# A graph network's adjacency built from subtiles of 5 nodes with one tile of 128 edges each, their rows gathered once a chunk from a table of overlapping rows

## The chip, the cores and the metric

The kernel runs on one NeuronCore of a Trainium2 chip. The metric is the device time of one execution in microseconds, as the median of 11 runs. The engines are called as the profile calls them: PE (TensorE; PEld is its weight load), DVE (VectorE), ACT (ScalarE), POOL (GpSimd) and SP (SyncE, which here only issues DMAs). Sixteen DMA engines move the data.

## The reference

Four graph layers run over the same graph, each with a residual and a layer norm. There are N = 6250 nodes with 128 features, and E = 100000 edges, whose list is sorted by destination.

```python
edge_index = jnp.stack([src, dst])
x = _layernorm(x + _L0_gnn_ref(x, edge_index, L0_gnn_W_l, L0_gnn_b_l, L0_gnn_W_r), axis=-1)
x = _layernorm(x + _L1_gnn_ref(x, edge_weight1, ..., src, dst, edge_type_8), axis=-1)
x = _layernorm(x + _L2_gnn_ref(x, edge_index, ...), axis=-1)
x = _layernorm(x + _L3_gnn_ref(x, edge_index, edge_attr_16, ...), axis=-1)
```

Layer 0, in whose stage the change lies, takes the mean of `x[src]` over the edges of each destination, multiplies it with `W_l`, adds a bias and `x @ W_r`, and normalizes the rows. Layer 1 sums messages by relation, layer 2 runs five gated steps, each with a sum over the same edges, and layer 3 is an edge network with a sum by source.

## The kernel before

The kernel has two routes. A preparation (`gnn_kernel`) looks at the edge list, works out tables, and sets a flag; a regular graph like this one then takes the route `even`, any other the route `general`.

**Dense and sparse nodes.** The 6250 nodes are 49 tiles of 128 (`NT`). They go in steps of 768 nodes: 4 tiles, called a chunk, are summed by a dense product, and 2 tiles by lists of edges. There are 8 dense chunks of 512 destinations (`DW`) and 17 listed tiles. The sum of a dense chunk is a product with its adjacency, a count matrix of 128 source rows by 49 source tiles by 512 destinations in bf16. Layer 0 builds these 8 matrices, uses each once (`dense0`), and stores it in DRAM (`stored`, `adj_d`) for layer 2's five steps.

**How an adjacency is built.** A chunk is cut into 43 subtiles of `U = 12` destination nodes. The edges into one subtile fit into `US = 256` places, that is two tiles of 128 edges. For each edge the preparation has written a record of two numbers into `rec_d`: a key of source tile and destination, and the source's place in its tile. `block_load` reads for a block of up to 11 subtiles (`SU`) the starts of the edges (`start_d`, a register load on SP) and then the 256 records of each subtile, one DMA each; all of this is on SP's queue. `block_keys` subtracts the subtile's offset (L931) and compares the places with 0 to 127 into one-hots `ohs` (L935), both on DVE. `hot_keys` makes for each edge tile a one-hot `ohk` over 600 columns (50 source tiles by 12 nodes, L943, DVE). `subtile` multiplies the two on PE (L958): two edge tiles by two halves of 300 columns make four matmuls, which add up in a PSUM tile of two banks, of which there are two. ACT copies the 600 columns into the chunk's `stage` (L960).

**What stands beside it.** For a listed tile, `fetch0` gathers 128 messages by an indirect DMA on POOL (L754, 10 buffers, 8 ahead), `hot0` makes a one-hot on DVE (L1002), and `sparse0` multiplies them (L1011). `dense0` multiplies three bf16 parts of x with the stage, 147 matmuls of 512 columns a chunk (L980). `post` does the rest of layer 0 for a chunk, and then layer 1's products `fhw` (L1095) with their stores. `counts` works out the edges per node.

**What sets the order.** Each engine works its queue in order. In layer 0 that order is written by hand: pieces of work get a place in a list (`events`), counted in chunks, and `play` issues them sorted by it. A chunk's adjacency is built in one such period, while `dense0` works on the chunk before, so there are nine periods: the first only builds, the last only uses. In the preparation the order comes from a scheduler when the kernel is built. It puts `rec_d<-rec` on SP's queue behind 11 of the 13 loads of x, whose parts are then made by ACT and POOL and written to `x_in`. The first instructions of `even` wait for the last of these writes.

Of the kernel before, what the change touches and what calls it, by code (L numbers as in the profile page):

```python
# [34 lines left out]
U = 12  # L35
US = 256
SU = 11
DW = 512
SLOTS = 18
NU = (N + U - 1) // U  # L40
RL = 200
RQ = EC // RL
QR = P - 1
NQ = 5 * QR
KH = (NT + 1) // 2
# [617 lines left out]
def even(ctx: ExitStack, tc: tile.TileContext, a, out, rec_d, start_d, list_d, x_in, ends):  # L663
# [115 lines left out]
    with tc.tile_pool(name="f0", bufs=1) as l0, \  # L779
# [5 lines left out]
        start = l0.tile([1, NQ + P], I32, name="start")  # L785
# [23 lines left out]
        def list_load(i):  # L809
            t, n = sparse[i][0], len(sparse[i])  # L810
            dst_ls[i] = dst_l = l0.tile([P, 2, SLOTS], I32, tag="dst_l", bufs=3, name=f"dst_l{i}")
            _, at = nc.values_load_multi_w_load_instructions(
                start[0:1, NQ + t:NQ + t + n], engines=[ET.SP], min_val=0, max_val=E,
                skip_runtime_bounds_check_because="counts of edges, none above their number")
            for j in range(n):
                for to, k in ((src_l[:, 2 * i + j, :], 0), (dst_l[:, j, :], 1)):
                    nc.sync.dma_start(to, list_d[k, bass.ds(at[j], SLOTS * P)].rearrange("(p s) -> p s", p=P))
# [82 lines left out]

        iota_k = l0.tile([P, KH * 2 * U], FP16, name="iota_k")
        nc.gpsimd.iota(iota_k, pattern=[[1, KH * 2 * U]], base=0, channel_multiplier=0,
                       allow_small_or_imprecise_dtypes=True)
        iota_u = l0.tile([P, SU], F32, name="iota_u")
        nc.gpsimd.iota(iota_u, pattern=[[1024, SU]], base=0, channel_multiplier=0,
                       allow_small_or_imprecise_dtypes=True)


        each = -(-DW // U)
        blocks = [(d, ts[0] * P // U + u, min(SU, each - u)) for d, ts in enumerate(dense) for u in range(0, each, SU)]  # L910
        recs, keys, ohss, stages, hot, msgs, sums, aggT, parts = ({} for _ in range(9))

        def block_load(i):
            if i >= len(blocks):
                return
            d, b, n = blocks[i]
            recs[b] = rec = l0.tile([P, SU, 2, 2], F32, tag="recs", bufs=4, name=f"recs{b}")
            _, at = nc.values_load_multi_w_load_instructions(
                start[0:1, b:b + n], engines=[ET.SP], min_val=0, max_val=E,
                skip_runtime_bounds_check_because="counts of edges, none above their number")  # L920
            for u in range(n):
                nc.sync.dma_start(rec[:, u, :, :].rearrange("p j r -> p (j r)"),
                                  rec_d[bass.ds(at[u], US), :].rearrange("(p j) r -> p (j r)", p=P))

        def block_keys(i):
            if i >= len(blocks):
                return
            d, b, n = blocks[i]
            rec = recs.pop(b)
            keys[b] = key = l0.tile([P, SU, 2], F32, tag="key", bufs=3, name=f"key{b}")  # L930
            nc.vector.scalar_tensor_tensor(key[:, :n, :], rec[:, :n, :, 0], float(-1024 * b),  # L931
                                           iota_u[:, :n].unsqueeze(2).to_broadcast([P, n, 2]),
                                           op0=ALU.add, op1=ALU.subtract)
            ohss[b] = ohs = l0.tile([P, 2 * SU, P], BF16, tag="ohs", bufs=2, name=f"ohs{b}")
            nc.vector.tensor_tensor(ohs[:, :2 * n, :], iota_h.unsqueeze(1).to_broadcast([P, 2 * n, P]),  # L935
                                    rec.rearrange("p u j r -> p (u j) r")[:, :2 * n, 1:2].to_broadcast([P, 2 * n, P]),
                                    op=ALU.is_equal)

        def hot_keys(b, u):
            ks = []  # L940
            for j in range(2):
                ohk = l0.tile([P, 2 * KH * U], BF16, tag="ohk", bufs=5, name=f"ohk{b}_{u}_{j}")
                nc.vector.tensor_scalar(ohk, iota_k, keys[b][:, u, j:j + 1], None, op0=ALU.is_equal)  # L943
                ks.append(ohk)
            hot[b, u] = ks

        def subtile(d, b, u, after):

            if after:
                hot_keys(*after)  # L950
            if d not in stages:
                stages[d] = l0.tile([P, 2 * KH, DW], BF16, tag="stage", bufs=2, name=f"stage{d}")
            c = (b + u) * U - dense[d][0] * P
            w = min(U, DW - c)
            p = ps(f"adj_p{b}_{u}", "adj", 2, 1024)
            for j, ohk in enumerate(hot.pop((b, u))):
                for q in range(2):
                    nc.tensor.matmul(p[:, q * 512:q * 512 + KH * U], ohss[b][:, 2 * u + j, :],  # L958
                                     ohk[:, q * KH * U:(q + 1) * KH * U], start=(j == 0), stop=(j == 1))
            nc.scalar.copy(stages[d][:, :, c:c + w].rearrange("p (q b) d -> p q b d", q=2),  # L960
                           p.rearrange("p (q n) -> p q n", q=2)[:, :, :KH * U]
                           .rearrange("p q (b d) -> p q b d", d=U)[:, :, :, :w])
# [27 lines left out]
        def fetch0(k):  # L990
            if k >= len(hots):
                return
            i, j = hots[k]
            msgs[k] = msg = l0.tile([P, 3 * D], BF16, tag="msg", bufs=10, name=f"m0_{k}")
            gather(msg, x_in, src_l[:, i, j:j + 1])
# [8 lines left out]
        def sparse0(k):  # L1004
            i, j = hots[k]
            fetch0(k + 8)
# [102 lines left out]
        with tc.manual_schedule(engines=FOUR):  # L1109
            list_load(0)  # L1110
            block_load(0)
            list_load(1)
            block_load(1)
            load_weights()
            list_locs(0)
            block_keys(0)
            for k in range(8):
                fetch0(k)
            for k in range(6):
                hot0(k)  # L1120
            order = [(d, b, u) for d, b, n in blocks for u in range(n)]
            hot_keys(*order[0][1:])
# [3 lines left out]
            for d in range(len(dense)):  # L1126
                mine = [o for o in order if o[0] == d]
                for k, (_, b, u) in enumerate(mine):
                    t = d + (k + 0.5) / len(mine)
                    g = order.index((d, b, u))  # L1130
                    nxt = order[g + 1][1:] if g + 1 < len(order) else None
                    i = [x[1] for x in blocks].index(b)
                    if u == 0 and i:
                        events.append((t - 1e-6, lambda i=i: block_load(i + 1)))
                    if u == 7:
                        events.append((t - 2e-6, lambda i=i: block_keys(i + 1)))
                    events.append((t, lambda d=d, b=b, u=u, nxt=nxt: subtile(d, b, u, nxt)))
# [945 lines left out]
def gnn_kernel(ctx: ExitStack, tc: tile.TileContext, a, out):  # L2083
# [4 lines left out]
    rec_d = dram.tile([E + US, 2], F32, name="rec_d")  # L2088
    start_d = dram.tile([NQ + P], I32, name="start_d")
# [7 lines left out]
    with tc.tile_pool(name="prep", bufs=1) as prep, \  # L2097
# [13 lines left out]
        for p0, p1 in ((0, 112), (112, EP)):  # L2111
# [9 lines left out]
        NR = NQ // QR + 1  # L2121
        node = prep.tile([P, NR * P], F32, name="node")
        nc.gpsimd.iota(node[:, :(NR - 1) * P], pattern=[[U * QR, NR - 1], [U, P]], base=0, channel_multiplier=0,
                       allow_small_or_imprecise_dtypes=True)
        nc.gpsimd.iota(node[:, (NR - 1) * P:], pattern=[[P, P]], base=0, channel_multiplier=0,
                       allow_small_or_imprecise_dtypes=True)
        own = prep.tile([P, NR], F32, name="own")
        nc.gpsimd.iota(own[:, :NR - 1], pattern=[[U * QR, NR - 1]], base=0, channel_multiplier=U,
                       allow_small_or_imprecise_dtypes=True)
        nc.gpsimd.iota(own[:, NR - 1:], pattern=[[0, 1]], base=0, channel_multiplier=P,  # L2130
                       allow_small_or_imprecise_dtypes=True)
# [29 lines left out]
        p_t = psum.tile([P, 512], F32, name="p_t")  # L2161
# [6 lines left out]
        nc.sync.dma_start(start_d[:NQ].rearrange("(r c) -> r c", c=QR), at_i[:NR - 1, :QR])  # L2168
        nc.sync.dma_start(start_d[NQ:].rearrange("(o n) -> o n", o=1), at_i[NR - 1:, :])

# [8 lines left out]
        nc.vector.tensor_scalar(miss, p_t[:NR, P:2 * P], float(E * U // N) / U, float(E), op0=ALU.mult, op1=ALU.min)  # L2179
# [7 lines left out]
        nc.vector.tensor_scalar(most, most, float(NR - 1), float(SLOTS * P - US), op0=ALU.is_equal, op1=ALU.mult)  # L2187
        nc.vector.tensor_scalar(most, most, float(US), None, op0=ALU.add)
        room = prep.tile([NR, QR], F32, name="room")
        nc.vector.tensor_sub(room, at[:, 1:], at[:, :QR])  # L2190
# [54 lines left out]
        q = pre("q")  # L2245
        nc.vector.tensor_scalar(q, d_f[:, :EC], 1.0 / U, -(U - 1) / (2.0 * U), op0=ALU.mult, op1=ALU.add)
        nc.vector.tensor_scalar(q, q, BIG, None, op0=ALU.add)
        nc.vector.tensor_scalar(q, q, -BIG, None, op0=ALU.add)
        v = pre("v")
# [81 lines left out]
```

## Time and profile before

| what | value |
| --- | --- |
| median of 11 runs | 7677.67 us (7668.8 to 7686.42) |
| profiled execution, its own time | 7692.67 us |
| span of its trace | 7690.9 us |
| mean granted TensorE clock | 0.865 |
| PE busy | 6054.7 us (79%), 26053 instructions |
| DVE, ACT, POOL busy | 2896.0, 2422.4, 4291.6 us |
| preparation, to the first instruction of `even` | 0 to 76.03 us |
| first product of an adjacency (L958) | 98.72 us |
| first product with an adjacency (L980) | 176.4 us |
| layer 0's last stores issued | 866 us |

The trace was taken from one profiled execution, whose own time is 15.0 us (0.2%) over the median. Times in it are counted from the start of its span. A group's row gives the line, the engine, the operation with its output and inputs, how often it came, the busy time and the mean of one in ns, and then the idle time ahead of it on its engine. Layer 0 is the first 870 us of 7691; what comes after it (layer 1, the five steps of layer 2, layer 3) is not touched by the change.

### The profile page before, as it was taken

How to read it: one execution, taken by the hardware profiler on the slowest of the kernel's cores; microseconds unless marked ns; L12 is line 12 of the kernel's file. 1: busy time of each engine (PE TensorE's matmuls, PEld its weight loads, DVE VectorE, ACT ScalarE, POOL GpSimd, SP SyncE). 2: the span in 40 equal slices, each digit the busy share in tenths (PEclk: the TensorE clock that was granted, in tenths of full speed). 3: DMA queues.
4: the chain of work that ended last, by engine and by line, in shares of the span. 5: the costliest groups of instructions: out<-in, count | busy, mean ns of one | idle time of the engine just before them, and what ended most of it. 6: DMA issues, size and time to landing. Idle time of an engine off the chain costs nothing.

```text
span 7690.9 us, 84421 instructions
## 1 busy us (share of the span) xinstructions
PE 6054.7 (79%) x26053; PEld 4173.2 (54%) x26053; DVE 2896.0 (38%) x8862; ACT 2422.4 (31%) x3623; POOL 4291.6 (56%) x4463
## 2 busy tenths in 40 slices
PE   4899666777588888887888888887888877777777
PEld 2455344455355566665666565665665554555455
DVE  6667343555233222221222222222222245555555
ACT  2344111111055433332333233332332223333333
POOL 5655466666556555555555555555554325555554
PEclk6999776766599899998999999998999988888888
DMA  4778533333477866686666766676665533333222
GB/s 125 209 230 243 166 129 123 120 115 112 123 227 246 282 220 215 201 276 205 213 205 223 268 213 204 222 239 208 209 210 178 163 104 80 81 83 84 79 81 64
DMA packets 809494, 1341.36 MB, mean 174 GB/s; under 512 B 166327, under 2 KB 430493, under 8 KB 809036
## 3 DMA queue, kind: packets, MB, share of 16 engines
q1 hardware_dynamic: 555260, 693.60, 28.5%
q0 software_dynamic: 206192, 553.93, 23.8%
q10 hardware_dynamic: 47584, 88.33, 3.1%
q8 instruction: 213, 3.49, 0.2%
q14 instruction: 245, 2.01, 0.1%
HBM read 1032.07 MB, written 303.32 MB: 174 GB/s over the span
## 4 chain that ended last, share of the span: by engine, by line
PE 63%; issue 11%; another core or an unknown queue 10%; DVE 7%; DMA 3%; ACT 3%; POOL 1%; SPq 1%; ACTq 0%; DVEq 0%; POOLq 0%
PE ag_p L1453 19%; PE r L1537 5%; PE z L1537 5%; PE sp_p L1485 4%; PE sum L1374 3%; PE h L1537 2%; PE s_p L1909 2%; PE i L1537 2%; PE ag_p L980 2%; PE m_p L1874 2%; PE h_p L1859 2%; DMA m<-tab,src_l 2%; PE adj_p L958 2%; PE g_rank L2045 1%
## 5 line engine op out<-in xcount | busy, mean ns | idle before, releaser
L1453 PE MATMUL ag_p<-af,hs 128*128 128x512 f32 x7056 | 2186.2, 434 | 363.9 <-issue 215.4
L754 POOL DMA_INDIRECT m<-tab,src_l x1530 | 1478.2, 966 | 1533.6 <-PE ag_p L1453 590.6
L1453 PEld LDWEIGHTS ag_p<-af,hs 128*128 128x128 f32 x7056 | 1364.9, 200 | 824.7 <-issue 402.0
L1424 ACT CAST af<-ab 128x1024 fp32r<-128x1024 bf16 (+1 forms) x1000 | 1016.7, 1027 | 1291.4 <-PE ag_p L1453 374.5
L754 POOL DMA_INDIRECT f_m<-by_dst,f_ix x819 | 800.8, 978 | 611.4 <-issue 289.3
L754 POOL DMA_INDIRECT fm<-f_hw,turned_hw x782 | 775.0, 991 | 408.8 <-issue 154.1
L1622 POOL DMA_INDIRECT rec_d<-f_rec,row x782 | 776.6, 993 | 243.8 <-issue 234.2
L1475 DVE TENSOR_SCALAR s<-iota_h,loc_l 128x128 fp32r<-128x128 f16 x1530 | 405.2, 298 | 1007.4 <-PE ag_p L1453 408.3
L1485 PE MATMUL sp_p<-m,s 128*128 128x512 f32 (+1 forms) x1530 | 690.2, 451 | 109.1 <-DMA m<-tab,src_l 64.8
L1374 PE MATMUL sum<-fs,fm 128*128 128x128 f32 (+13 forms) x1924 | 410.1, 367 | 114.0 <-DVE fs L1365 47.8
L754 POOL DMA_INDIRECT m<-x_in,src_l x306 | 349.6, 1142 | 264.8 <-PE sp_p L1011 153.5
L1374 PEld LDWEIGHTS sum<-fs,fm 128*128 128x128 f32 x1924 | 361.8, 273 | 196.1 <-issue 97.5
L1485 PEld LDWEIGHTS sp_p<-m,s 128*128 128x128 f32 x1530 | 306.0, 200 | 250.9 <-issue 177.2
L1344 ACT COPY f_rec<-ap_p 128x512 f32<-128x512 f32 x196 | 108.0, 588 | 704.4 <-issue 296.4
L980 PE MATMUL ag_p<-stage,xs 128*128 128x512 bf16 x1176 | 324.1, 388 | 3.7 <-ACT aT L987 2.2
L960 ACT CAST stage<-adj_p 128x600 bf16<-128x600 f32 (+1 forms) x344 | 223.9, 654 | 325.3 <-PE adj_p L958 212.9
L1866 DVE TENSOR_TENSOR dT<-h_p,dT 128x512 f32<-128x512 f32 (+1 forms) x208 | 141.5, 680 | 482.4 <-remote 174.7
L1551 DVE SCALAR_TENSOR_TENSOR r<-h,fc_b_hh,r 128x256 f32<-128x256 f32 (+2 forms) x170 | 101.7, 600 | 577.6 <-PE h L1537 358.3
L958 PE MATMUL adj_p<-ohk,ohs 128*128 128x300 bf16 x1376 | 249.3, 307 | 72.0 <-DVE ohk L943 53.8
L1365 DVE TENSOR_SCALAR fs<-f_iota_n,loc,turned_wgt 128x128 f32<-128x128 f32 x782 | 242.7, 356 | 131.9 <-PE sum L1374 83.7
L1909 PE MATMUL s_p<-f_s,f_ms 128*128 128x128 f32 (+1 forms) x1638 | 279.3, 314 | 11.6 <-issue 10.3
L1559 ACT ACTIVATE z<-z,f_brz 128x256 f32<-128x256 f32 (+2 forms) x170 | 96.6, 568 | 600.3 <-PE z L1537 486.2
(386 smaller groups left out, 9126.4 us busy)
## 6 DMA issues: line engine op xcount, KB each, us to landing
ab<-adj_d SPq DMA_DIRECT2D x960, 256.0 KB
f_rec<-edge_d SPq DMA_DIRECT2D x391, 130.0 KB
rg<-rec_d SPq DMA_DIRECT2D x195, 260.0 KB
edge_d<-f_rec SPq DMA_DIRECT2D x97, 520.0 KB
adj_d<-stage SPq DMA_DIRECT2D x56, 896.0 KB
tab<-r ACTq DMA_DIRECT2D x196, 256.0 KB
hs<-tab SPq DMA_DIRECT2D x28, 1792.0 KB
xs<-x_in SPq DMA_DIRECT2D x56, 672.0 KB
```

The costliest lines, as they stand in the source:

```text
L754: nc.gpsimd.indirect_dma_start(out=dst, out_offset=None, in_=table, in_offset=bass.IndirectOffsetOnAxis(ap=idx, axis=0))
L958: nc.tensor.matmul(p[:, q * 512:q * 512 + KH * U], ohss[b][:, 2 * u + j, :], ohk[:, q * KH * U:(q + 1) * KH * U], start=(j == 0), stop=(j ...
L980: nc.tensor.matmul(sums["d", d], parts[d, g][:, s % XG, q, :], stages[d][:, s, :], start=(s == 0 and q == 0), stop=(s == NT - 1 and q == 2))
L1365: nc.vector.tensor_scalar(s, iota_n, loc[:, k:k + 1], wgt[:, k:k + 1], op0=ALU.is_equal, op1=ALU.mult)
L1374: nc.tensor.matmul(sums[c][:, x0 - c0:x1 - c0], msg, s[:, x0 - w0:x1 - w0], start=False, stop=(k == last_k[c]))
L1424: nc.scalar.copy(af[:, :m, :], abs_.pop((layer, d, g))[:, :m, :])
L1453: nc.tensor.matmul(sums[layer, d, k], hs[:, s, q, k, :], afs[layer, d, g][:, s % SG, :], start=(s == 0 and q == 0), stop=(s == NT - 1 and ...
L1475: nc.vector.tensor_scalar(s, iota_h, loc_l[:, i, j:j + 1], None, op0=ALU.is_equal)
L1485: nc.tensor.matmul(p[:, :2 * w], hot.pop((layer, k)), msgs.pop((layer, k))[:, :2 * w], start=(j == 0), stop=(j == SLOTS - 1))
L1537: nc.tensor.matmul(p[:, :n], w[:, k, ms], src, start=(start and i == 0), stop=(stop and i == len(ks) - 1))
L1622: st = nc.gpsimd.indirect_dma_start(out=rec3_d, out_offset=bass.IndirectOffsetOnAxis(ap=row3[:, c:c + 1], axis=0), in_=recs[c // CB][:, c ...
L1909: nc.tensor.matmul(sums[c][:, a0:a1], ms[:, j * P:(j + 1) * P], s[:, :a1 - a0], start=False, stop=(stop and j == m - 1))
```

## The change

A subtile now has 5 nodes and one tile of 128 edges, so a chunk has 103 subtiles (`NSUB`), and the matmul of one is 245 columns (5 nodes by 49 source tiles). Two subtiles share a PSUM tile of one bank, of which there are three, and one copy on ACT. The one-hots `ohs` are made for 22 subtiles at once.

The records of a chunk are no longer read subtile by subtile. The preparation writes, for each of the 8 chunks, a table `rec_t[d]` in DRAM: row k holds the 128 records from edge `from_t[d] + 8 k` on, 1024 bytes, so that neighbouring rows overlap by 120 records. A table has 1213 rows, and each is made by one DMA from DRAM to DRAM on SP's queue. One indirect gather on POOL (`chunk_rows`) then fetches the 103 rows that begin at (up to 7 records before) the subtiles' first edges, a row per partition; two transposes on PE and two DVE instructions (`chunk_keys`) turn them, so that edges lie on partitions. The preparation looks up 10 tiles of starts where it looked up 6.

`rec_d` and the lists are written by two DMAs each, of 112 and of 13 rows, where one had 125. In SP's queue `rec_d` and the 8 tables now stand ahead of the last 4 of the 13 loads of x. The messages of the listed tiles have 13 buffers and are fetched 11 ahead.

```diff
-U = 12
-US = 256
-SU = 11
+U = 5
+US = 128
+AL = 8
+SU = 22
...
+NSUB = -(-DW // U)
+DP = 768
...
-        def block_load(i):
...
-            _, at = nc.values_load_multi_w_load_instructions(
-                start[0:1, b:b + n], engines=[ET.SP], min_val=0, max_val=E,
...
-            for u in range(n):
-                nc.sync.dma_start(rec[:, u, :, :].rearrange("p j r -> p (j r)"),
-                                  rec_d[bass.ds(at[u], US), :].rearrange("(p j) r -> p (j r)", p=P))
...
+        def chunk_rows(d):
+
+            if d < len(dense):
+                recs[d] = rec = l0.tile([P, US, 2], F32, tag="recs", bufs=2, name=f"recs{d}")
+                gather(rec.rearrange("u e r -> u (e r)"), rec_t[d], row_t[:, d:d + 1])
+
+        def chunk_keys(d):
+            if d < len(dense):
+                rec = recs.pop(d)
+                p = ps(f"key_p{d}")
+                for r in range(2):
+                    nc.tensor.transpose(p[:, r * P:(r + 1) * P], rec[:, :, r], ident)
...
+        def hot_keys(d, u):
+            hot[d, u] = ohk = l0.tile([P, KN], BF16, tag="ohk", bufs=8, name=f"ohk{d}_{u}")
+            nc.vector.tensor_scalar(ohk, iota_k.rearrange("p n t -> p (n t)"), keys[d][:, u:u + 1], None, op0=ALU.is_equal)
...
-            p = ps(f"adj_p{b}_{u}", "adj", 2, 1024)
-            for j, ohk in enumerate(hot.pop((b, u))):
-                for q in range(2):
-                    nc.tensor.matmul(p[:, q * 512:q * 512 + KH * U], ohss[b][:, 2 * u + j, :],
-                                     ohk[:, q * KH * U:(q + 1) * KH * U], start=(j == 0), stop=(j == 1))
...
+            p = ps(f"adj_p{d}_{us[0]}", "adj", 3)
+            for i, u in enumerate(us):
+                nc.tensor.matmul(p[:, i * KN:(i + 1) * KN], ohss[d, u // SU * SU][:, u % SU, :], hot.pop((d, u)),
+                                 start=True, stop=True)
+            c0, c1 = us[0] * U, min(us[-1] * U + U, DW)
+            nc.scalar.copy(stages[d][:, :, c0:c1], p[:, :len(us) * KN].rearrange("p (n t) -> p t n", t=NT)[:, :, :c1 - c0])
...
-            fetch0(k + 8)
+            fetch0(k + 11)
...
+            chunk_rows(0)
             list_load(0)
-            block_load(0)
             list_load(1)
-            block_load(1)
             load_weights()
+            chunk_keys(0)
+            block_hots(0, 0)
             list_locs(0)
-            block_keys(0)
...
+                events.append((d + 0.3, lambda d=d: chunk_rows(d + 1)))
+                events.append((d + 0.75, lambda d=d: chunk_keys(d + 1)))
...
+    rows_t = (2 * SLACK + (NSUB - 1) * U * (E // N)) // AL + 1
+    from_t = [max(0, d * DP * (E // N) - SLACK) for d in range(8)]
+    rec_t = [dram.tile([rows_t, US * 2], F32, name=f"rec_t{d}") for d in range(8)]
...
-        nc.sync.dma_start(rec_d[:E, :].rearrange("(p c) r -> p c r", p=EP), rec)
...
+        for p0, p1 in ((0, 112), (112, EP)):
+            nc.sync.dma_start(rec_d.rearrange("(p c) -> p c", p=EP)[p0:p1, :], rec[p0:p1].rearrange("p c r -> p (c r)"))
+        for d in range(8):
+            o = 2 * from_t[d]
+            part = rec_d[o:o + 2 * AL * (rows_t - 1) + 2 * US]
+            nc.sync.dma_start(rec_t[d], bass.AP(tensor=part.tensor, offset=part.offset, ap=[[2 * AL, rows_t], [1, 2 * US]]))
```

## The prediction

> **What bounds the kernel now.** I read the stretches first, then the order on PE, the groups of layer 0, and last the DMA view of the preparation. The change touches only the first 870 us. Stretches (columns after the bounds and length: busy us and instructions of PE, PEld, DVE, ACT, POOL, then the granted clock, the DMA share and GB/s):
>
> ```profile
> 98.00:185.00 87.00, 54.28 (x334) 31.50 (x334) 59.98 (x190) 31.23 (x49) 57.22 (x50) 0.74 0.46 126
> 185.00:773.00 588.00, 522.02 (x2875) 292.75 (x2876) 408.42 (x1295) 254.92 (x445) 322.67 (x281) 0.96 0.77 226
> 773.00:871.00 98.00, 84.26 (x369) 43.02 (x368) 30.82 (x118) 29.53 (x60) 18.40 (x23) 0.94 0.65 211
> ```
>
> In the middle stretch, seven periods, PE is busy 89%, DVE 69%, the DMA engines 77%: PE bounds it, with 66 us idle. In the first period nothing is full. How long a product holds PE is read from successive starts:
>
> ```profile
> 703.90 0.33 PE L1011 MATMUL sp_p<-m,s 128*128 128x384 bf16 x1
> 704.06 0.68 PE L958 MATMUL adj_p<-ohk,ohs 128*128 128x300 bf16 x4
> 704.58 0.81 PE L980 MATMUL ag_p<-stage,xs 128*128 128x512 bf16 x3
> 705.22 0.33 PE L1011 MATMUL sp_p<-m,s 128*128 128x384 bf16 x1
> ```
>
> Four products of 300 columns hold PE for 0.52 us (704.06 to 704.58), 0.13 each; three of 512 for 0.64. It goes by columns. The groups, from 98 to 870 us:
>
> ```profile
> L958 PE MATMUL adj_p<-ohk,ohs 128*128 128x300 bf16 x1376 | 249.3, 307 | 72.0 <-DVE ohk L943 53.8 <-ACT stage L960 11.6 <-issue 6.1
> L943 DVE TENSOR_SCALAR ohk<-iota_k,key 128x600 bf16<-128x600 f16 x686 | 239.5, 381 | 111.0 <-PE adj_p L958 82.0 <-issue 11.2 <-PE sp_p L1011 10.9
> L960 ACT CAST stage<-adj_p 128x600 bf16<-128x600 f32 x336 | 220.0, 658 | 321.3 <-PE adj_p L958 210.2 <-issue 30.3 <-DMA recs<-rec_d 26.2
> L1002 DVE TENSOR_SCALAR s<-iota_h,loc_l 128x128 bf16<-128x128 f16 x300 | 77.7, 260 | 2.4 <-PE sp_p L1011 2.4
> L935 DVE TENSOR_TENSOR ohs<-iota_h,recs 128x2816 bf16<-128x2816 f16 x23 | 70.9, 3082 | 0.0
> ```
>
> The end of the preparation, and the queue of SP's DMAs in three windows of it (packets, MB, share of 16 engines): 2 to 5 us (loads, nearly all of 112 rows), 62.5 to 66.5 us (the write of `rec_d`, 125 rows of 6400 bytes) and 68 to 69.6 us (the last load of x, 106 rows of 512 bytes):
>
> ```profile
> 59.31 0.30 SPq L2258 DMA_DIRECT2D rec_d<-rec  x1
> 59.70 0.37 SPq L2271 DMA_DIRECT2D xin<-in_x  x1
> ...
> 69.22 0.62 ACT L2278 CAST xin<-xin 128x512 bf16<-128x512 f32 x1 [15.03 <-DMA xin<-in_x]
> ...
> 76.03 0.20 POOL masks.py:197 MEMSET f_ident<- 128x128 f32 x1 [1.84 <-DMA x_in<-xin]
> ```
> ```profile
> q1 hardware_dynamic: 408, 0.74, 81.9%
> ```
> ```profile
> q1 hardware_dynamic: 71, 0.45, 32.5%
> ```
> ```profile
> q1 hardware_dynamic: 136, 0.07, 14.3%
> ```
>
> This is the reading that decides. 32.5% of 16 is 5.2 engines for 125 rows, 14.3% is 2.3 for 106 rows, 81.9% is 13.1 for 112 rows. 125 is 5 x 25, 106 is 2 x 53, 112 is 16 x 7: a transfer runs on as many engines, up to 16, as divide its rows. And a load of x issued at 59.70, right behind the 125 rows, lands only at 69.22: its shares on the five engines stand behind the write.
>
> **Part 1, the tables.** Eight transfers of 1213 rows of 1024 bytes. 1213 is prime. By the rows above each has one engine. Whether the eight share it the trace shows only for smaller ones: from 6.2 to 9.3 us two list writes of 125 rows, both issued by then, are under way, and the share is 32.8%, five engines and not ten. So I put all eight on one. Bytes: 8 x 1213 x 1024 = 9.94 MB. Pace of one engine: 114 GB/s over 5.2 engines = 21.9 GB/s (6400-byte rows); 43 GB/s over 2.3 = 18.8 (512-byte rows); over the whole run ACT's queue moved 88.33 MB in 3.1% of 16 x 7690.9 us = 3815 us, 23.2 GB/s (1.9 KB a packet). No row goes from DRAM to DRAM. I take 21.9, as 1024 bytes lie between the others: **454 us**, with ends 429 and 529.
>
> [...]
>
> Nothing covers this time. Behind the tables on SP's queue are four loads of x, each with a sixteenth of its rows on that engine; behind them ACT, POOL, the last write of `x_in`, for which all engines wait at 76.03, and with it all of `even`.
>
> Times: the records are ready about as before. DVE loses 3 x 0.56 + 0.98 us (q, v), gains four counts of 0.49 and 1.5 us of wider comparisons; POOL gains four lookups of 1.25 us, ahead of x parts that are not last. +1 us, 60.3. `rec_d` on 16 engines: 0.78 MB at 247 GB/s, 3.2 us, landed at 64.5. Tables until 518.5. Loads of x land from 520.5 on. Then before it took 6.8 us (69.22 to 76.03) for two blocks, now four, 3.3 us each by POOL's starts at 42.43, 45.67, 49.03: 13.4. `even` starts at 534 instead of 76: **+458**.
>
> **Part 2, the start and the first period.** First product at 98.72, 22.7 us after `even` begins, behind SP's list and block loads. Now: POOL's constants 2.95, the gather 0.95 and some 2 to land, two transposes of 0.28, keys 0.35, `ohs` 3.08, one-hots 2: 12. Gain 10. The building period took 77.7 us (98.72 to 176.4); POOL's 38 fetches and 16 lookups at 1.25 give 67. Gain 8 (0 to 11).
>
> **Part 3, seven periods.** PE: 1376 x 0.13 = 179 us become 824 products of 245 columns, 0.106 each, 87 us: 92 off, 80 of them here; 16 transposes at 0.28 come back, 4. PE's weight loads mean 102 ns, just under 106, so they stay hidden; if not, PE pays only the difference. DVE: `ohk` 381 ns at 600 columns and 260 at 128 are 0.256 ns a column, so 290 at 245: 824 x 0.290 = 239 for 688 x 0.381 = 262; `ohs` 824 x 128 x 1.095 ns = 116 for 96; together about -6 with the keys. ACT: 658 ns at 600, 567 at 490 by 0.825 ns a column (493 at 400): 416 copies, 233 for 225; if strided reading doubled it, ACT would still be at 550 of 700. POOL: 8 gathers more, 9 us, with 398 of 773 busy; behind each stand `m` gathers that are 11 ahead. SP loses 344 loads at 0.52 and 32 register loads at 2.57, 261 us, but PE waits for no transfer in this stretch but 1.1 us of `xr`, so nothing more is earned. What is late next: the DMA share, 77%, goes to 87% if the same bytes move in 520 us, and DVE to 78%. Of 76 net I take 50 (0 to 76, as far as these two allow).
>
> **Sum.** 458 - 10 - 8 - 50 = +390. On the profiled execution 7692.67 + 390 = 8083; it stands 15.0 us over the median, so the forecast is 7677.67 + 390 = **8068 us**. Ends: 433 - 10 - 11 - 76 = +336 with a little more for idle PE gone, 7985; 533 - 0 = +533 and a few us of delay, 8225.
>
> **Rivals.** (a) The tables use all sixteen engines, because a DRAM-to-DRAM transfer is cut differently from those seen. Then 454/16 = 28 us, `even` starts at 108, +32, and 32 - 68 = -36: 7642, faster. It decides from eight engines up: with four the tables take 114 us and the sum is still +50, with seven it is about zero. For it: no such transfer is in the trace. Against it: 125, 112 and 106 rows. (b) One engine, but the odd run of 245 sends `ohk` to the slow form of DVE: by `ohs` 1.095 ns a column in place of 0.256, +0.206 each, +169 us on DVE, in all 499 (the stretches' sum) - 6 + 169 = 662 of 700, and the periods gain nothing: +440, 8118. No odd run of 2-byte numbers is in the trace. (c) DRAM to DRAM on one engine costs reading and writing in turn, 908 us: +844, 8522. Against it: the paces of loads and writes are alike, so both sides seem to overlap.
>
> [...]
>
> **How the numbers follow.** My forecast 0.70, (b) 0.10, (c) 0.06, (a) 0.14. The first two lie in 7985 to 8225. 0.2%, about 15 us, is what a measurement of this kernel can tell from no change. Of (a), 0.11 is faster, 0.02 the same and 0.01 slower; all else is slower: 0.11, 0.02, 0.87.
>
> **What would show it.** Right: from about 65 to 520 us a DMA share near 0.06 and some 22 GB/s, all compute engines idle, the first L958 product (now another line) near 546 us, and layer 0 after that about 70 us shorter, with PE's products of the adjacency near 0.106 us apart. Wrong: a share over 0.2 while the tables move, or `even` starting before 200 us; a period of 84 us again with DVE over 85% busy would be (b).

## The result, and the profile after

The changed kernel takes 8067.04 us (median of 8 runs, 8051.46 to 8084.91), the kernel before 7674.98 us beside it (31 runs): the ratio is 1.051, with a 95% interval of 1.0497 to 1.0523, and the difference 392 us. The forecast was 8068 us. The profiled execution shown here took 8094.4 us, its span is 8092.3 us, its granted clock 0.838.

The order of time in the preparation, SP's queue and what follows it (start, length, engine, line; the bracket is the idle time before and what ended it):

```profile
49.93 0.78 SPq L2261 DMA_DIRECT2D rec_d<-rec  x2
54.07 359.91 SPq L2265 DMA_DIRECT2D rec_t<-rec_d  x8
414.08 54.04 SPq L2279 DMA_DIRECT2D xin<-in_x  x3
...
471.36 0.62 ACT L2286 CAST xin<-xin 128x512 bf16<-128x512 f32 x1 [414.60 <-DMA xin<-in_x]
...
483.06 0.20 POOL masks.py:197 MEMSET f_ident<- 128x128 f32 x1 [1.83 <-DMA x_in<-xin]
```

SP's own issues are held: the eight tables need 360 us of them. The first load of x behind them lands at 471 us, and the layer starts at 483.06 instead of 76.03. From 66 to 469 us nothing computes (busy us of PE, PEld, DVE, ACT, POOL, then clock, DMA share, GB/s), and SP's queue shows one engine's worth of work: the first row is that stretch, the second the DMA view from 104 to 440 us (packets, MB, share of 16 engines), the third the spread of single issues (least, median and greatest in ns):

```profile
66.00:469.00 403.00, 0.00 (x0) 0.00 (x0) 0.00 (x0) 0.00 (x0) 0.00 (x0) 0.50 0.08 26
```
```profile
q1 hardware_dynamic: 7914, 8.10, 6.8%
```
```profile
L2265 SPq DMA_DIRECT2D rec_t<-rec_d x8: 722/51418/52471, 54.1 to 362.6; - x8
```

6.8% of 16 is 1.09 engines, and 8.10 MB in 336 us are 24 GB/s. One table takes 51.4 us.

Layer 0 itself: its first product, two successive pairs of products later on, and the groups of the adjacency from 483 to 1250 us:

```profile
495.38 0.57 PE L951 MATMUL adj_p<-ohk,ohs 128*128 128x245 bf16 x2 [5.13 <-DVE ohk L941]
```
```profile
930.00 0.37 PE L951 MATMUL adj_p<-ohk,ohs 128*128 128x245 bf16 x2
930.21 0.33 PE L1003 MATMUL sp_p<-m,s 128*128 128x384 bf16 x1
```
```profile
L951 PE MATMUL adj_p<-ohk,ohs 128*128 128x245 bf16 x824 | 175.2, 295 | 103.8 <-DVE ohk L941 74.7 <-issue 23.7 <-DVE fsq L772 3.6
L941 DVE TENSOR_SCALAR ohk<-iota_k,key 128x245 bf16<-128x245 f16 x824 | 197.9, 299 | 27.6 <-PE adj_p L951 11.2 <-remote 6.4 <-issue 4.4
L954 ACT CAST stage<-adj_p 128x490 bf16<-128x490 f32 (+1 forms) x416 | 230.1, 565 | 295.6 <-PE adj_p L951 207.9 <-remote 31.8 <-issue 21.3
L936 DVE TENSOR_TENSOR ohs<-iota_h,low 128x2816 bf16<-128x2816 f16 (+1 forms) x40 | 115.9, 2896 | 0.0
```

Two products hold PE for 0.21 us, 0.105 each. What PE waits for has grown: 74.7 us on `ohk`, 53.8 before.

From the first to the last dense product the eight chunks took 645.4 us, before 665.1 (the rows give the least, median and greatest length in ns, and the first and last start; the kernel before comes first):

```profile
L980 PE MATMUL ag_p<-stage,xs x1176: 376/379/634, 176.4 to 841.5; 128*128 128x512 bf16 x196
```
```profile
L972 PE MATMUL ag_p<-stage,xs x1176: 376/379/634, 577.7 to 1223.0; 128*128 128x512 bf16 x196
```

From here on the periods are counted from the first dense product; the period ahead of it, which only builds, is called the building period. The next rows are the third to the seventh period, first of the kernel before, then of the changed one:

```profile
370.60:789.90 419.30, 387.94 (x2100) 218.53 (x2100) 283.54 (x883) 196.56 (x343) 215.01 (x189) 0.98 0.80 237
```
```profile
779.70:1171.40 391.70, 344.68 (x1762) 188.99 (x1762) 270.48 (x960) 197.48 (x388) 234.00 (x191) 0.93 0.75 244
```

PE is busy 43 us less, but the time is only 28 us shorter: PE's idle time went from 31 to 47 us, at a lower clock.

### The profile page after: what moved, and what is told of

It is laid out like the page before. It is cut to its first block, busy times and chain, and to the rows that moved or that the text cites. A ratio compares the mean times of both kernels' runs of the same rounds, so it can differ in the third digit from the quotient of the medians.

```text
span 8092.3 us, 82092 instructions
## 1 busy us (share of the span) xinstructions
PE 6022.8 (74%) x25535; PEld 4139.7 (51%) x25535; DVE 2869.6 (35%) x8998; ACT 2424.0 (30%) x3695; POOL 4330.9 (54%) x4485
## 4 chain that ended last, share of the span: by engine, by line
PE 61%; issue 10%; another core or an unknown queue 9%; DVE 7%; DMA 3%; ACT 2%; POOL 1%; SPq 0%; ACTq 0%; DVEq 0%; POOLq 0%
PE ag_p L1447 19%; PE r L1531 5%; PE z L1531 5%; PE sp_p L1479 4%; PE sum L1368 3%; PE h L1531 2%; PE s_p L1903 2%; PE i L1531 2%; PE ag_p L972 2%; PE m_p L1868 2%; DMA m<-tab,src_l 2%; PE h_p L1853 2%; PE g_rank L2039 1%; PE d_p L1828 1%
## 5 line engine op out<-in xcount | busy, mean ns | idle before, releaser
L754 POOL DMA_INDIRECT m<-x_in,src_l x306 | 369.2, 1207 | 222.4 <-PE adj_p L951 90.8
L954 ACT CAST stage<-adj_p 128x490 bf16<-128x490 f32 (+1 forms) x416 | 230.1, 565 | 295.6 <-PE adj_p L951 207.9
L1868 PE MATMUL m_p<-f_hs,fw_L_gnn_eW 128*128 128x512 f32 (+1 forms) x416 | 242.4, 667 | 46.2 <-ACT mT L1870 23.2
```

Source lines behind the costliest of these rows:

```text
L754: nc.gpsimd.indirect_dma_start(out=dst, out_offset=None, in_=table, in_offset=bass.IndirectOffsetOnAxis(ap=idx, axis=0))
L1868: nc.tensor.matmul(p_m[:, :e], e2[:, 0, :], held[i].pop("hs")[:, :e], start=True, stop=True)
```

## The experiments

The runs of the experiments fell on four chips. The kernel before took 6683 us beside the first four, 7688 beside the next four, 6679 beside the ninth and tenth, and 7749 beside the last (its granted clock was 0.92 on the first of these chips and 0.86 on the second). So only ratios and differences within a group are compared, and the absolute times in the expectations, worked out from 7675, are read as differences.

**The number of engines.** One more row, 1214 = 2 x 607, and three more, 1216 = 16 x 76:

```diff
-    rows_t = (2 * SLACK + (NSUB - 1) * U * (E // N)) // AL + 1
+    rows_t = (2 * SLACK + (NSUB - 1) * U * (E // N)) // AL + 2                    # 1214
+    rows_t = -(-((2 * SLACK + (NSUB - 1) * U * (E // N)) // AL + 1) // 16) * 16   # 1216
```

> Each of the 8 tables gets 1214 rows (2 x 607) in place of 1213 (prime); nothing else changes, and 0.08% more bytes move. Theory (a transfer runs on as many engines as divide its rows): two engines in place of one. In the changed kernel the eight took about 414 us (51.4 us each by SP's issues); here 207 us, issues of about 26 us, a DMA share near 0.13 in place of 0.068, the first instruction of the layer near 483 - 207 = 276 us, and a time near 8067 - 207 = 7860 us. Rival (the price is one per row, about 42 ns, whatever the engines, or is set by SP, whose issues of 51 us hold it): no change, 8067 us, share 0.068.

> Each table gets 1216 rows (16 x 76), 0.25% more bytes. Theory: all sixteen engines. 414/16 = 26 us if each engine keeps its 24 GB/s, 40 us if they move together only the 247 GB/s that the 16 engines showed for records; the layer starts at 95 to 110 us; the rest of the layer keeps the 26 us that it gained in the changed kernel, so 7675 + (95..110 - 76) - 26 = 7668 to 7683 us, about the kernel before. Rival (a price per row, or SP): 8067 us. Second rival (the gain of 26 us came only from the rest during the 430 idle us): 7694 to 7709 us.

With 1214 rows the kernel took 6871.0 us (one run), 188 us over the kernel before (185 expected); the layer started at 279.1 us. With 1216 rows it took 6689.34 us, a ratio of 1.0013 (1.0004 to 1.0022), and the layer started at 105.8 us; as a ratio, the theory had 0.999 to 1.001 and its second rival 1.0025 to 1.0044, so the time lies just above the one and below the other. SP's queue while the tables move, from 80 to 240 us and from 58 to 88 us:

```profile
q1 hardware_dynamic: 7516, 7.68, 13.5%
```
```profile
q1 hardware_dynamic: 8663, 8.76, 93.8%
```

1.09, 2.16 and 15.0 engines for 1213, 1214 and 1216 rows, and issues of 51.4, 25.7 and 4.1 us. Three rows more take nearly the whole loss back; what is left is the time that sixteen engines need for the same bytes (the layer starts at 105.8 us, and at 70.6 without tables, as the next experiment shows). A price per row is excluded.

**No tables.** The gather takes its index in steps of 8 records, 64 bytes, and reads 1024 bytes from there; so it can read `rec_d` itself:

```diff
-    rows_t = (2 * SLACK + (NSUB - 1) * U * (E // N)) // AL + 1
-    from_t = [max(0, d * DP * (E // N) - SLACK) for d in range(8)]
-    rec_t = [dram.tile([rows_t, US * 2], F32, name=f"rec_t{d}") for d in range(8)]
+    rows_t = (E - US) // AL + 1
+    from_t = [0] * 8
+    rec_t = [rec_d.rearrange("(n r) -> n r", r=2 * AL)] * 8
...
-        for d in range(8):
...
-            nc.sync.dma_start(rec_t[d], bass.AP(tensor=part.tensor, offset=part.offset, ap=[[2 * AL, rows_t], [1, 2 * US]]))
```

> No tables: the gather of a chunk reads its 103 rows of 1024 bytes straight from the records, taken as rows of 64 bytes by index, each read running on over the 16 that follow. Theory (only the copying of the tables costs): the loads of x follow the records at once, the layer starts at 54 + 2 + 13 = 69 us (before 76), the first dense product 95 us later, the eight chunks take 645 us (before 665): 7675 - 7 - 6 - 20 = 7642 us, between 7632 and 7655. Rival (the 26 us that the layer gained came from the rest before it): 7668 us. Rival (reading the records at odd offsets is slow, so that each gather holds POOL or comes late): more than 7675 us, with the key transposes waiting for recs.

6655.04 us, ratio 0.9959 (0.9945 to 0.9973), 28 us faster than the kernel before. SP passes on from the records to the loads of x, and the layer starts at 70.59 (the forecast ratio, by its 7632 to 7655 us, was 0.9944 to 0.9974):

```profile
50.17 0.78 SPq L2261 DMA_DIRECT2D rec_d<-rec  x2
51.05 5.69 SPq L2275 DMA_DIRECT2D xin<-in_x  x3
63.80 0.26 SPq L2278 DMA_DIRECT2D xin<-in_x  x1
...
70.59 0.20 POOL masks.py:197 MEMSET f_ident<- 128x128 f32 x1 [1.81 <-DMA x_in<-xin]
```

The gathers of the records took 954 ns each, as from the tables. So the layer gains without the long rest before it, and the gather needs no copies.

**The tables inside the layer.** 1213 rows again, but each table copied a period before its use:

```diff
+            chunk_table(0)
             chunk_rows(0)
...
-                events.append((d + 0.3, lambda d=d: chunk_rows(d + 1)))
-                events.append((d + 0.75, lambda d=d: chunk_keys(d + 1)))
+                events.append((d + 0.02, lambda d=d: chunk_table(d + 1)))
+                events.append((d + 0.8, lambda d=d: chunk_rows(d + 1)))
+                events.append((d + 0.9, lambda d=d: chunk_keys(d + 1)))
```

> Tables of 1213 rows as in the changed kernel, but copied inside the layer: that of chunk 0 at its start, each further one at the beginning of the period before its use (51 us of one engine in a period of some 80), and gathered at 0.8 of that period. Theory A (the copying only has to be off the path): the layer starts at 71 us, its first product comes 51 us later, the rest as without tables: 6655 + 51 = 6706 us. Theory B (every transfer has a sixteenth of its rows on that engine and queues behind the table, and SP is held by the issue): up to 51 us of each period are lost, at most 8 x 51 = 408 us, the time lies between 6760 and 7075 us, and waits for DMA appear in the periods.

8017.78 us (one run) where the kernel before took 7688: 330 us more. Without tables it would be 7657 there (0.9959), so 361 us are lost, near the upper end of theory B. They are not lost as B had it, a part in each period: the first product came 52 us later, the first chunk's period took 421 us, and the six after it 75 to 96. SP's queue, and the waits from 212 to 560 us:

```profile
128.39 0.68 SPq L917 DMA_DIRECT2D rec_t<-rec_d  x1
129.18 57.09 SPq L1166 DMA_DIRECT2D rec_d<-fill  x1
...
197.37 2.31 SPq L917 DMA_DIRECT2D rec_t<-rec_d  x1
199.73 57.23 SPq L1041 DMA_DIRECT2D xr<-in_x  x1
```
```profile
DVE nextT L888 <- DMA nextT<-node_d: 314.9, 1, 314.9
POOL grow L754 <- DVE grow L870: 314.4, 1, 314.4
```

The place in the written order does not bind SP. It ran ahead of the compute engines and issued one table after the other from 71 to 486 us, each with a held issue behind it. A small load of the count of edges (`nextT`) stood behind them and stopped DVE, POOL and PE for 315 us. A place in the list was no time on a queue that waited for nothing: the last table was issued at 486 us, and the last gather came at 1031.

**The changed kernel and the kernel before, once more, on one chip**, unedited:

> The changed kernel itself, beside the others of this study, on a chip that grants PE more clock (the kernel before took 6683 us there). Theory (one engine copies 1213 rows): the layer starts near 483 us as in its first profile, and with 1214 rows at 279 us and 6871 us the whole takes 6871 + 204 = 7075 us. The first building period took 82.3 us in the first profile, but 62 to 64 in the three kernels with more engines or no tables. Theory A (chip and clock): 63 us here as well. Theory B (the long one-engine copying leaves something behind that slows the first periods): 82 us, and 20 to 30 us more in the whole time, 7100 us.

> The kernel before, for its profile on the same chip: the layer starts at 76 us. Its first period and the eight chunks took 77.7 and 665 us in its first profile. If the chip alone made the first periods of the other kernels short, about 60 and 645 us here, and the gain of the eight chunks against 625 us is 20 us again; if not, 77 and 665 us, and the gain is 40 us.

8062.89 us, ratio 1.0506 (1.0469 to 1.0543); the layer starts at 483.4 and 76.3 us. The chip was not that of the first four runs, so the two theories are not told apart in the way that was planned. The building period took 74.7 us with the changed kernel (82.3 in its first profile) and 78.2 with the kernel before (77.7), but 62 to 64 in all four kernels on the first chip; there is no profile of the kernel before from there. Neither theory had 74.7. The eight chunks took 648.0 and 672.3 us. The next run settles a part: it has no tables (and fetches 8 messages ahead, not 11) and ran on this chip. Its building period took 69.0 us and its first two periods 210.5, which with tables took 74.7 and 204.4 here. So the first two periods are just as long without tables, and nothing that the copying leaves behind is needed for that; for the building period some 6 us stay open, between single executions.

**The lookahead of the messages**, without tables:

```diff
-            msgs[k] = msg = l0.tile([P, 3 * D], BF16, tag="msg", bufs=13, name=f"m0_{k}")
+            msgs[k] = msg = l0.tile([P, 3 * D], BF16, tag="msg", bufs=10, name=f"m0_{k}")
...
-            fetch0(k + 11)
+            fetch0(k + 8)
```

> As the one without tables, but the listed tiles' messages with 10 buffers and 8 ahead, as in the kernel before, in place of 13 and 11. Theory (the lookahead is not what shortened the periods): within 5 us of the one without tables (ratio 0.9959 to the kernel before). Rival (POOL, which has 8 gathers more, needs the lookahead so as not to make PE wait for messages): the chunks take 10 to 20 us longer, ratio 0.998 to 0.999.

Ratio 0.9963 (0.9944 to 0.9981), where 0.9959 was expected; the upper end of the interval just reaches the 0.998 of the rival. The third to the seventh period took 392.0 us, with 11 ahead 391.7 on the first chip: the lookahead does nothing there. The eight chunks took 654.1 us. That is 29 more than the 625.0 on the first chip, but only 6 more than the changed kernel took with 11 ahead on this one (648.0), so it doesn't speak for the rival.

**What holds the periods.** Two edits on the kernel without tables. One spreads the count of edges:

```diff
+            cat = [0.01, 0.38, 1.0, 1.75, 2.6, 3.5, 4.4]
             for b in range(NT // CN):
-                events += counts(b, 0.01 + 0.37 * b, 0.01 + 0.37 * min(b + 1, NT // CN - 1) + 0.66)
+                events += counts(b, cat[b], cat[min(b + 1, NT // CN - 1)] + 0.66)
```

> As the one without tables, with the seven pieces of the count of edges per node spread over the periods: they begin at 0.01, 0.38, 1.0, 1.75, 2.6, 3.5 and 4.4 chunks in place of every 0.37. Theory (the first periods, 95, 100.5 and 101.5 us in the changed kernel against 75 to 80 later, are long because the count's round trips POOL - DVE - PE - DVE - POOL stand in the queues between the adjacency's pieces): periods 0 to 2 lose some 30 us together, the later ones get some 12 back: 18 us less than without the spread, 7624 us. Rival (they are long because PE's clock is low there, 0.57 to 0.83, or because of the fetches): within 5 us of the one without the spread.

6655.68 us, ratio 0.9953 (0.9939 to 0.9967): no difference from the one without the spread. In the trace the first two periods fell from 181.8 to 162.7 us and the next five rose from 391.7 to 401.0; the layer also began 3.8 us later, for a reason that is not shown. That the pieces of the count lengthen the first two periods is shown, but not that their round trips do it alone: of the 19 us, 11 are busy time of PE (144.74 to 133.60) that moved on with 64 of its instructions, and 8 are idle time. The forecast gain did not come: in the total the rival's number was right.

The other edit makes the one-hots three pairs ahead of their products:

```diff
-            for u in order[0][1]:
-                hot_keys(0, u)
+            for e, us in order[:3]:
+                for u in us:
+                    hot_keys(e, u)
...
-                    g = order.index((d, us)) + 1
+                    g = order.index((d, us)) + 3
```

> As the one without tables, with the one-hots ohk made three pairs of subtiles ahead of their products on DVE's queue in place of one (the 8 buffers hold four pairs). Theory (the eight chunks gave only 17 to 24 us of the 50 forecast because PE now reaches each product earlier and waits for its one-hot, which stands behind the instructions of the layer's end on DVE: 40 us of such waits in five periods where the kernel before had 19 in four): the waits fall to some 10 us, the eight chunks take 20 to 30 us less than without this edit, and the ratio to the kernel before is 0.9920 to 0.9935 (0.9959 without). Rival (DVE in its fixed order is the pace, and a later waiting place takes over): chunks within 5 us, ratio 0.995 to 0.997.

6616.57 us, ratio 0.9907 (0.9891 to 0.9924). The theory had 0.9920 to 0.9935, so the gain is at least what it forecast. The chunks took 594.8 us, where they took 625.0 without this edit (on another chip, with the kernel before at 6683 us there and 6679 here). Without it the third to the seventh period took 391.7 us with PE busy 344.68, just as in the changed kernel. With it, these periods read as in the first row; the rows behind it are what PE waits for in them (us, times, longest), without and with the edit:

```profile
321.40:686.90 365.50, 336.02 (x1762) 188.79 (x1762) 269.99 (x959) 195.66 (x388) 219.59 (x192) 0.96 0.80 262
```
```profile
PE adj_p L951 <- DVE ohk L941: 40.4, 23, 3.6
```
```profile
PE adj_p L951 <- DVE ohk L941: 17.3, 10, 2.5
```

26 us less in five periods with the same work: the waits for `ohk` fall by 23 us, PE's idle time from 47 to 29 us, and PE's busy time by 9 us, with a granted clock of 0.96 in place of 0.93.

Both together:

> As the one with the one-hots three pairs ahead, and the seven pieces of the count spread over the periods as in the earlier run. Theory (with the one-hots ahead the later periods have room for the pieces): 10 us less than without the spread, ratio 0.991. Rival (what the first periods win the later ones lose, as in the earlier run, where periods 0 and 1 won 19 us and 2 to 5 lost 10): the same within 5 us.

6604.95 us (6597.74 to 6607.13, against 6613.13 to 6622.71 without the spread), ratio 0.9889 (0.9873 to 0.9906): 74 us faster than the kernel before, and the best version. The first two periods took 152.8 us for 177.8, the next five 374.0 for 365.5: more is won than lost, and 12 us of it reach the end.

The spread alone, in the kernel before:

> The kernel before (subtiles of 12 nodes, no tables), with only the seven pieces of the count spread over the periods as in the two runs with the spread. It tells how much of the best version is owed to the spread alone. Theory (in the kernel before PE has no room in the later periods, where it is 94 to 95 per cent busy, so that what the first periods win the later ones lose): within 8 us of the kernel before, ratio 0.999 to 1.001. Rival (the first periods win 25 us and the later ones take it without loss): ratio 0.996 to 0.998.

7738.85 us, ratio 0.9987 (0.9969 to 1.0006), no difference that the runs can tell. So the best version does not owe its 1.1% to the spread alone. One-hots further ahead were not tried in the kernel before, so how much they would give without the new subtiles is open.

## Why the prediction was right, point by point

The forecast of +390 us met a measured +392, and the mechanism of the loss held. That the two numbers agree within 2 us is luck: the start of the layer was forecast 51 us too late, and the gains in the building period and the chunks some 30 to 40 us too large. Changes in us, by the two pairs of profiles (the first two executions, and the repeated ones on one chip):

| step | forecast | first pair | repeated pair |
| --- | --- | --- | --- |
| start of the layer | +458 | +407.0 | +407.1 |
| from there to the first product | -10 | -10.4 | -9.7 |
| building period | -8 | +4.6 | -3.5 |
| the eight chunks | -50 | -19.8 | -24.3 |
| everything behind them | 0 | +19.9 | -5.1 |
| sum | +390 | +401.4 | +364.5 |

- **One engine for 1213 rows, queued on the same one, with nothing to cover it: right.** Share (1.09 engines), pace (24 GB/s) and the two runs with other numbers of rows (2.16 and 15.0 engines) show it; rival (a), all sixteen engines, becomes true with 1216 rows. Rival (c), half the pace, is refuted by 24 GB/s.
- **The pace was mis-sized.** 21.9 GB/s was taken from rows of 6400 bytes; the tables moved at 24.2 (9.94 MB in eight times 51.4 us), above even the 23.2 that was the fast end. From the records' landing to the first load of x it was 417 us, where 456 was forecast: 39 us too many. From there to the start of `even` it was 12 us for 13.
- **The records were ready 10 us earlier than forecast**, as the issue at 49.93 shows (60.3 was forecast). The forecast had counted the instructions that go and that come, and not the comparisons of another chain (`same`) that stand between the steps towards the records. Before and after:

```profile
43.84 0.56 DVE L2248 TENSOR_SCALAR q<-q 125x800 f32<-125x800 f32 x1
44.33 2.83 DVE L2205 TENSOR_SCALAR same<-bins 125x800 bf16<-125x800 bf16 x3
47.08 0.98 DVE L2250 SCALAR_TENSOR_TENSOR v<-q,d_f 125x800 f32<-125x800 f32 x1
```
```profile
48.52 0.90 DVE L2213 TENSOR_SCALAR same<-bins 125x800 bf16<-125x800 bf16 x3
49.35 0.56 DVE L2259 CAST rec<-l_i 125x800 f32<-125x800 int32 x1
```

  Three of them took 2.83 us before and 0.90 now. Ahead of the records stand 36 in place of 39, so hardly fewer, but together they took 21.9 us in place of 32.1. That is the 10 us; why they were shorter is not shown.
- **The start of `even` to the first product: right**, 12.3 us for 12. POOL's constants, the gather, the two transposes and the keys came as summed.
- **The building period: not as forecast.** It was to get 8 us shorter; it got 4.6 longer in one pair and 3.5 shorter in the other. The cause is not settled.
- **The unit prices of part 3 were right**: 0.105 us a product for 0.106, 299 ns an `ohk` for 290, 565 ns a copy for 567, 115.9 us of `ohs` for 116. Rival (b), 0.206 us more for each `ohk` of 245 columns, is refuted by the 299 ns.
- **What they are worth was mis-sized: 20 to 24 us for 50.** Spread evenly, 14 of the 50 belong to the first two of the seven periods and 36 to the next five. The five gave 28 us (29 in the repeated pair). The first two, which the next rows show before and after, became 8 us longer (5 in the repeated pair), so most of the gap lies there:

```profile
176.40:370.60 194.20, 158.49 (x921) 87.97 (x921) 136.95 (x456) 70.31 (x121) 123.07 (x107) 0.93 0.70 203
```
```profile
577.70:779.70 202.00, 147.68 (x789) 78.02 (x788) 130.35 (x492) 72.32 (x140) 126.43 (x112) 0.83 0.59 187
```

  The step that failed is "What is late next", which named the DMA share (87%) and DVE (78%). Neither filled: in the five periods DVE was busy 69% and the DMA share was 0.75. In the first two PE's idle time grew by 19 us: it waited for the count's `ended` 19.9 us where it had waited 4.3, and in the repeated pair 10.5 us for 6.1. In the five what came late was a distance: the one-hots stood one pair ahead of their product, two instructions of 0.3 us on a queue that also holds the layer's end. Four products of 300 columns had taken PE 0.52 us, two of 245 take 0.21; PE came sooner and waited. The run with three pairs ahead took 26 us off these five periods, and so shows it.
- **Everything behind layer 0** differs by +19.9 in one pair and -5.1 in the other, with the same instructions: this is how single executions vary, and it is why the two errors of the first pair end at +401 and not at +382.

## What to carry to other kernels

Before a transfer gets a shape, factor its row count: 1213 rows cost some 380 us that 1216 rows do not, and no engine's busy time shows it, only a DMA share of 6.8%, about a sixteenth, and issues that are held for 51.4 us. A gather that takes an index and a length may need no prepared table at all (954 ns each here, from the tables and from the records). And when an instruction gets shorter, look at how far ahead its input is made: here five periods got 28 us shorter with the operand queued one step ahead of its product, and 26 us more with three.

## What the runs showed of the hardware

An issue on SP behind a one-engine table lasted about as long as that table: 51.4 us for the tables among themselves, 48.18 us for a load of 64 KB that took 0.36 us elsewhere. So a table on one engine took its 51.4 us and held SP for about as long. One engine (1.09 by the DMA share) moved 24 GB/s from DRAM to DRAM in rows of 1024 bytes, two (2.16) 48, and sixteen (15.0), with the writes of `x_in` among them, 318 in the mean. And for the same 1762 instructions in five periods PE was granted a clock of 0.96 where it was idle for 29 us, and 0.93 where it was idle for 47 (the kernels with the one-hots three pairs and one pair ahead); which is the cause of the other no run shows.
